# Pairwise outer products with batch norm: long rows as tiles of one sample, tiles in order of store

## The chip, the core and the metric

The kernel runs on one core of a Trainium2 chip. TensorE multiplies matrices, VectorE (DVE), ScalarE (ACT) and GpSimd (POOL) work element by element, SyncE (SP) issues the transfers, and 16 DMA engines carry them out. The metric is the time of one execution on the device, in microseconds (us); lower is better.

## The reference, cut to what matters

```python
B, F = 1024, 39            # r_xi, r_xj: (1024, 39, 16) float32
rows, cols = np.tril_indices(39, k=-1)      # 741 pairs (row > col)
cross = xj[:, rows, :, None] * xi[:, cols, None, :]        # (1024, 741, 16, 16)
mean = jnp.mean(cross, axis=(0, 2, 3), keepdims=True)
var = jnp.mean(jnp.square(cross - mean), axis=(0, 2, 3), keepdims=True)
normed = (cross - mean) * rsqrt(var + 1e-5)
normed = normed * gamma[None, :, None, None] + beta[None, :, None, None]
out = normed[:, :, None, :, :] * W[None, None, :, :, :]
```

For each sample and each pair of fields (row r, column c < r) the kernel forms the 16x16 outer product of two vectors, normalizes it with that pair's statistics over all samples, applies gamma and beta, and multiplies it by W. Row r has r pairs. The output has 1024 x 741 x 256 floats, 777 MB; the inputs have 5.1 MB.

## The kernel before

The 128 partitions hold eight samples each (`NT` = 8). A short first part loads the inputs, computes the statistics of all pairs from sums and small matrix products, and leaves for each pair a scale s and a shift t in `st_sb`. Each output pair is then (s xi) outer xj + t, times W.

**Tiles and slots.** The results pass through one buffer, `y_sb`, with 152 slots for a pair (one KB per partition each). The list `tiles` has one entry for each piece of work: its rows, its first sample `t0`, its first slot, and a mark. Each tile holds T = 2 samples. A row r and the rows that fill up its lap, 38 - r and its neighbour, share the 152 slots; I call one filling of the buffer a lap. The order of the list is: row 19 (four tiles), rows 20 and 18 in turn, row 38, then for r = 37, 35, ... 23 and each two samples row r, row r - 1 and the group of the two short rows (38 - r, 39 - r), and last rows 21 and 17. The row r - 1 (and every other tile of rows 20 and 38) lies at the end of the buffer with its two samples in reversed order (the mark `slot`, read by `at_of`), although it is stored second.

**Work on a tile.** The main loop at the end of the kernel takes tile after tile. `scale_xi(n + 2)` makes s xi on GpSimd (L191) into one of two buffers of the pool `scaled`. `finish(n)` adds t and multiplies by W. `products(n + 1)` makes the outer products of the next tile. A product is one instruction for one sample and one of the 16 values of xj, over all pairs of the row (L168 on ScalarE, L170 on GpSimd): ScalarE makes the first `split`, GpSimd the others. GpSimd makes 4 of 16, 5 in rows over 33 (`LONG`), and 3 in rows 31 to 33 (`POOL_I_BESIDE`), whose laps hold rows 5 to 7, which GpSimd makes in one instruction a sample (L226, `OUTER` = 7). Rows 1 to 4 are made by VectorE (L207, L217).

In `finish`, VectorE adds and multiplies pair by pair in one instruction over the tile's samples (`stt`, L334). It leaves a few pairs to GpSimd: in rows over 33 eight pairs (`POOL_PAIRS_LONG`), whose t ScalarE adds (L318) and which GpSimd then multiplies by W in two instructions (L323); in shorter tiles 13% of the pairs, with both steps on GpSimd (L320, L323).

**Stores.** All stores go out on SP's queue, in the order of the program; `bounds` says after which pairs of a tile `finish` calls `store`. A store waits for the engines that wrote its pairs. A product of a later tile waits for the store that reads its slots. Nothing reorders instructions: each engine follows the program, and waits come from overlaps of what is read and written.

The first eight tiles have piece sizes of their own (`FIRST_PIECES`). Row groups' statistics are spread ahead of need (`due`, in tiles).

Of the kernel before, what the change touches and what calls it, by code (L numbers as in the profile page):

```python
# [7 lines left out]
F32 = mybir.dt.float32  # L8
# [6 lines left out]
T = 2  # L15
# [3 lines left out]
ONE, LONG, WHOLE = 30, 33, 36  # L19
FIRST_PIECES = (  # L20
    (0, 1, 3, 6, 10, 14, 19), (0, 4, 9, 14, 19), (0, 4, 11, 19), (0, 9, 19), (0, 10, 20), (0, 9, 18), (0, 10, 20), (0, 9, 18)
)


POOL_I, POOL_I_LONG, POOL_I_FIRST = 4, 5, (6, 6, 5)
POOL_SHARE, POOL_PAIRS_LONG, POOL_PAIRS_FIRST = 0.13, 8, 3

SHORT, OWN = 4, 1


OUTER, POOL_I_BESIDE = 7, 3


ROW_GROUPS = (
# [7 lines left out]
def tile_pair_outer_batchnorm(  # L42
# [16 lines left out]
    P = nc.NUM_PARTITIONS  # L59
    NB, F, E = xi.shape  # L60
    NT = NB // P
    EE = E * E
# [4 lines left out]

    half = T * (F - 1)
    mid = (F - 1) // 2
    tiles = [((mid,), t0, t0 // T * half // 2, 0) for t0 in range(0, NT, T)]  # L70
    slot = 0
    for r in (mid + 1, F - 1):
        for t0 in range(0, NT, T):
            tiles.append(((r,), t0, slot * (2 * half - T * r), slot))
            if r < F - 1:
                tiles.append(((F - 1 - r,), t0, half if slot else T * r, 0))
            slot ^= 1
# [5 lines left out]
    r = mid + 2  # L83
    for t0 in range(0, NT, 2 * T):
        tiles.append(((r,), t0, 0, 0))
        tiles.append(((r,), t0 + T, 2 * half - T * r, 1))
        tiles.append(((F - 1 - r,), t0, T * r, 0))
        tiles.append(((F - 1 - r,), t0 + T, T * (F - 1), 0))

    RAW = 1  # L90

# [55 lines left out]
    stt = nc.vector.scalar_tensor_tensor  # L147

    def view(n):
        rows, _, u, _ = tiles[n]  # L150
        return y_sb[:, u : u + T * sum(rows), :].rearrange("p (t n) e -> p t n e", t=T)

    def parts(n):
        at = 0
# [1 line left out]
            yield r, at, at + r  # L156
            at += r

    def at_of(n, t):
        return T - 1 - t if tiles[n][3] else t  # L160

    def product(n, r, at, engine, t, i, src):

        t0 = tiles[n][1]
        y = view(n)[:, at_of(n, t), at : at + r].rearrange("p n (i j) -> p n i j", j=E)[:, :, i, :]
        scale = xj_sb[:, t0 + t, r, i : i + 1]
        if engine is nc.scalar:
            nc.scalar.activation(y, src, AF.Copy, scale=scale)  # L168
        else:
            engine.tensor_scalar(y, src, scale, 1.0, ALU.mult, ALU.mult)  # L170
# [11 lines left out]
    xs_of = {}  # L182

    def scale_xi(n):
        rows, t0 = tiles[n][:2]
        if rows[-1] <= SHORT:
            return
        xs = scaled.tile([P, T, sum(rows), E], F32, tag="xs", name=f"xs_{rows[0]}_{t0}")
        for r, c0, c1 in parts(n):
            n0 = first[r]  # L190
            nc.gpsimd.tensor_tensor(  # L191
                xs[:, :, c0:c1, :],
                xi_sb[:, t0 : t0 + T, 0:r, :],
                s_sb[:, :, n0 : n0 + r, :].to_broadcast([P, T, r, E]),
                ALU.mult,
            )
        xs_of[n] = xs

    def products(n):

        t0 = tiles[n][1]
        xs = xs_of.pop(n, None)
        for r, c0, c1 in parts(n):
            outer = view(n)[:, :, c0:c1].rearrange("p t n (i j) -> p t n i j", j=E)
            if r <= SHORT:
                xs_r = scaled_short.tile([P, T, r, E], F32, tag="xs_short", name=f"xs_{r}_{t0}")
                nc.vector.tensor_tensor(  # L207
                    xs_r,
                    xi_sb[:, t0 : t0 + T, 0:r, :],
                    s_short[:, first[r] : first[r] + r]  # L210
                    .unsqueeze(1)
                    .unsqueeze(3)
                    .to_broadcast([P, T, r, E]),
                    ALU.mult,
                )
                for t in range(T):
                    nc.vector.tensor_tensor(  # L217
                        outer[:, t],
                        xs_r[:, t].unsqueeze(2).to_broadcast([P, r, E, E]),
                        xj_short[:, t0 + t, r - 1 : r, :].unsqueeze(3).to_broadcast([P, r, E, E]),  # L220
                        ALU.mult,
                    )
                continue
            if r <= OUTER:
                for t in range(T):
                    nc.gpsimd.tensor_tensor(  # L226
                        outer[:, t],
                        xs[:, t, c0:c1].unsqueeze(2).to_broadcast([P, r, E, E]),
                        xj_sb[:, t0 + t, r : r + 1, :].unsqueeze(3).to_broadcast([P, r, E, E]),
                        ALU.mult,  # L230
                    )
# [12 lines left out]
    def store(n, c0, c1, t_from=0, t_to=T):  # L244
        rows, t0 = tiles[n][:2]
        n0, r = first[rows[0]], sum(rows)

        whole = n >= len(FIRST_PIECES) and r <= WHOLE
        flipped = tiles[n][3]
        step = 1 if flipped or r > mid and (whole or c1 == r) else t_to - t_from  # L250
        for t in range(t_from, t_to, step):
            if whole and step == 1 and t == t_to - 1:
                if c1 < r:
                    continue
                c0 = 0
            nc.sync.dma_start(
                out_v[:, t0 + t : t0 + t + step, (n0 + c0) * EE : (n0 + c1) * EE],
                view(n)[:, at_of(n, t) : at_of(n, t) + step, c0:c1, :].rearrange("p t n e -> p t (n e)"),
            )

    def affine(n, pairs, engines=(nc.scalar, nc.gpsimd)):
# [25 lines left out]
    def bounds(n):  # L287
        if n < len(FIRST_PIECES):
            return FIRST_PIECES[n]
        rows = tiles[n][0]  # L290
        r = sum(rows)
        if r <= ONE or len(rows) > 1:
            return 0, r

        return 0, r // 2 + max(0, (WHOLE + 1 - r) * 3 // 2), r

    def finish(n):


        rows = tiles[n][0]  # L300
# [12 lines left out]
        for c0 in range(p0, p1, step):  # L313
            c1 = min(c0 + step, p1)
            for c in range(c0, c1):
                t_c = t_sb[:, n0 + c : n0 + c + 1]
                if long:
                    nc.scalar.activation(y[:, :, c, :], y[:, :, c, :], AF.Identity, bias=t_c)  # L318
# [4 lines left out]
            nc.gpsimd.tensor_tensor(  # L323
                y[:, :, c0:c1, :],
                y[:, :, c0:c1, :],
                w_sb.unsqueeze(1).to_broadcast([P, T, c1 - c0, EE]),
                ALU.mult,
            )

        size = 1 if n == RAW else T  # L330
        for t in range(0, T, size):
            for c0, c1 in zip(bounds(n), bounds(n)[1:]):
                for c in [*range(c0, min(c1, p0)), *range(max(c0, p1), c1)]:
                    stt(  # L334
                        y[:, t : t + size, c, :],
                        y[:, t : t + size, c, :],
                        t_sb[:, n0 + c : n0 + c + 1],
                        w_dve.to_broadcast([P, size, EE]),
                        ALU.add,
                        ALU.mult,  # L340
                    )
                store(n, c0, c1, t, t + size)
# [247 lines left out]
```

## Time and profile before

| | us |
|---|---|
| median of 3 runs | 1865.06 (1864.89 to 1865.09) |
| the profiled execution, its own time | 1865.3 |
| its span | 1863.6 |
| VectorE busy | 1713.5 (92%) |
| ScalarE busy | 1574.4 (84%) |
| GpSimd busy | 1530.3 (82%) |
| TensorE busy | 33.1 (2%) |

Busy time is the time in which an engine executes an instruction. The rows of groups give for each source line and shape the count, the busy time, the mean length of one and the idle time ahead of it with what ended it. The table of stretches gives the same for chosen pieces of the span. In the timeline a row is a run of like instructions, with its start, its length, and in brackets the engine's idle time before it and what ended that.

The waits, summed up by who waited for whom, begin with these (total us, times, longest):

```profile
ACT y_sb L168 <- DMA out_dram<-y_sb: 210.2, 82, 8.9
POOL xs L191 <- ACT y_sb L168: 171.1, 42, 8.7
POOL y_sb L323 <- ACT y_sb L318: 78.5, 20, 7.7
```

### The profile page before, as it was taken

How to read it: one execution, taken by the hardware profiler on the slowest of the kernel's cores; microseconds unless marked ns; L12 is line 12 of the kernel's file. 1: busy time of each engine (PE TensorE's matmuls, PEld its weight loads, DVE VectorE, ACT ScalarE, POOL GpSimd, SP SyncE). 2: the span in 40 equal slices, each digit the busy share in tenths (PEclk: the TensorE clock that was granted, in tenths of full speed). 3: DMA queues.
4: the chain of work that ended last, by engine and by line, in shares of the span. 5: the costliest groups of instructions: out<-in, count | busy, mean ns of one | idle time of the engine just before them, and what ended most of it. 6: DMA issues, size and time to landing. Idle time of an engine off the chain costs nothing. (4 is left out here: it accounts for less than half of the span.)

```text
span 1863.6 us, 9245 instructions
## 1 busy us (share of the span) xinstructions
PE 33.1 (2%) x212; PEld 32.3 (2%) x212; DVE 1713.5 (92%) x2642; ACT 1574.4 (84%) x3130; POOL 1530.3 (82%) x1627
## 2 busy tenths in 40 slices
PE   7000000000000000000000000000000000000000
PEld 6000000000000000000000000000000000000000
DVE  8999889898999999999999999989998999999994
ACT  8999889888888777777877989899988998999981
POOL 9999778777877688889888888879878888888882
PEclk7555555555555555555555555555555555555555
DMA  7999999999999999999999999999999999999999
GB/s 294 395 422 423 428 426 412 427 428 436 427 427 427 414 416 428 427 425 423 429 428 433 409 428 418 433 427 428 428 431 428 428 435 426 420 419 426 426 427 386
DMA packets 46822, 783.60 MB, mean 420 GB/s; under 512 B 4512, under 2 KB 5152, under 8 KB 12704
## 3 DMA queue, kind: packets, MB, share of 16 engines
q1 hardware_dynamic: 46464, 782.53, 98.7%
q10 hardware_dynamic: 288, 0.48, 0.1%
q14 instruction: 69, 0.57, 0.1%
q8 instruction: 1, 0.02, 0.0%
HBM read 6.00 MB, written 776.99 MB: 420 GB/s over the span
## 5 line engine op out<-in xcount | busy, mean ns | idle before, releaser
L334 DVE SCALAR_TENSOR_TENSOR y_sb<-y_sb,st_sb,w_dve 128x512 f32<-128x512 f32 (+1 forms) x2515 | 1652.3, 739 | 115.2 <-issue 61.1
L168 ACT ACTIVATE y_sb<-xs,xj_sb 128x576 f32<-128x576 f32 (+23 forms) x2930 | 1451.3, 587 | 241.6 <-DMA out_dram<-y_sb 210.2
L323 POOL TENSOR_TENSOR y_sb<-y_sb,w_sb 128x2048 f32<-128x2048 f32 (+2 forms) x131 | 508.5, 3888 | 86.1 <-ACT y_sb L318 78.5
L170 POOL TENSOR_SCALAR y_sb<-xs,xj_sb 128x320 f32<-128x320 f32 (+21 forms) x1006 | 556.9, 576 | 9.8 <-DMA out_dram<-y_sb 9.7
L191 POOL TENSOR_TENSOR xs<-xi_sb,st_sb 128x640 f32<-128x640 f32 (+33 forms) x135 | 182.9, 1362 | 194.0 <-ACT y_sb L168 171.1
L320 POOL TENSOR_SCALAR y_sb<-y_sb,st_sb 128x512 f32<-128x512 f32 x287 | 193.5, 691 | 6.9 <-ACT y_sb L168 6.9
L318 ACT ACTIVATE y_sb<-y_sb,st_sb 128x512 f32<-128x512 f32 x160 | 100.2, 708 | 3.8 <-POOL y_sb L170 2.1
L226 POOL TENSOR_TENSOR y_sb<-xs,xj_sb 128x1280 f32<-128x1280 f32 (+2 forms) x24 | 66.5, 2801 | 0.0
L217 DVE TENSOR_TENSOR y_sb<-xs,ps 128x256 f32<-128x256 f32 (+3 forms) x32 | 24.8, 818 | 0.6
L513 PE MATMUL ps<-y_sb 38*128 38x38 f32 (+37 forms) x76 | 15.3, 378 | 2.4 <-DVE y_sb L499 2.4
L513 PEld LDWEIGHTS ps<-y_sb 38*128 38x128 f32 x76 | 15.2, 309 | 2.5 <-POOL y_sb L170 2.5
L170 POOL TENSOR_SCALAR y_sb<-xi_sb,xj_sb 128x304 f32<-128x304 f32 x24 | 11.9, 513 | 0.0
L279 DVE TENSOR_TENSOR y_sb<-y_sb,w_dve 128x2048 f32<-128x2048 f32 (+4 forms) x6 | 10.8, 1840 | 0.5 <-POOL y_sb L272 0.5
L390 DVE TENSOR_REDUCE y_sb<-y_sb 128x38 f32<-128x608 f32 x14 | 10.4, 780 | 0.0
L272 POOL TENSOR_SCALAR y_sb<-y_sb,st_sb 128x512 f32<-128x512 f32 x9 | 7.0, 793 | 1.6 <-ACT y_sb L168 1.6
L387 ACT ACTIVATE y_sb<-xj_sb 128x608 f32<-128x608 f32 x8 | 5.7, 709 | 1.1 <-DMA xj_sb<-in_r_xj_dram 0.7
L387 ACT ACTIVATE y_sb<-xi_sb 128x608 f32<-128x608 f32 x8 | 5.7, 706 | 1.1 <-DMA xi_sb<-in_r_xi_dram 0.8
L270 ACT ACTIVATE y_sb<-y_sb,st_sb 128x512 f32<-128x512 f32 x9 | 6.5, 804 | 0.1
L405 PE MATMUL ps<-xi_sb,y_sb 128*128 128x152 f32 x40 | 5.8, 295 | 0.1
L405 PEld LDWEIGHTS ps<-xi_sb,y_sb 128*128 128x128 f32 x40 | 5.5, 193 | 0.3 <-issue 0.3
L427 PE MATMUL ps<-y_sb 128*128 128x128 f32 x24 | 5.5, 428 | 1.0 <-POOL y_sb L345 1.0
L390 DVE TENSOR_REDUCE y_sb<-xi_sb 128x38 f32<-128x608 f32 x2 | 1.6, 785 | 4.0 <-DMA xi_sb<-in_r_xi_dram 4.0
(43 smaller groups left out, 54.1 us busy)
## 6 DMA issues: line engine op xcount, KB each, us to landing
out_dram<-y_sb SPq DMA_DIRECT2D x20, 2944.0 KB, 15.4
out_dram<-y_sb SPq DMA_DIRECT2D x24, 2432.0 KB, 12.8
out_dram<-y_sb SPq DMA_DIRECT2D x16, 3456.0 KB, 17.2
out_dram<-y_sb SPq DMA_DIRECT2D x12, 3968.0 KB, 19.6
out_dram<-y_sb SPq DMA_DIRECT2D x10, 4608.0 KB, 15.5
out_dram<-y_sb SPq DMA_DIRECT2D x12, 3840.0 KB, 20.5
out_dram<-y_sb SPq DMA_DIRECT2D x16, 2816.0 KB, 16.8
out_dram<-y_sb SPq DMA_DIRECT2D x12, 3072.0 KB, 14.4
```

Source lines behind the costliest of these rows:

```text
L168: nc.scalar.activation(y, src, AF.Copy, scale=scale)
L170: engine.tensor_scalar(y, src, scale, 1.0, ALU.mult, ALU.mult)
L191: nc.gpsimd.tensor_tensor(xs[:, :, c0:c1, :], xi_sb[:, t0 : t0 + T, 0:r, :], s_sb[:, :, n0 : n0 + r, :].to_broadcast([P, T, r, E]), ALU.mult,)
L217: nc.vector.tensor_tensor(outer[:, t], xs_r[:, t].unsqueeze(2).to_broadcast([P, r, E, E]), xj_short[:, t0 + t, r - 1 : r, :].unsqueeze(3). ...
L226: nc.gpsimd.tensor_tensor(outer[:, t], xs[:, t, c0:c1].unsqueeze(2).to_broadcast([P, r, E, E]), xj_sb[:, t0 + t, r : r + 1, :].unsqueeze(3 ...
L318: nc.scalar.activation(y[:, :, c, :], y[:, :, c, :], AF.Identity, bias=t_c)
L320: nc.gpsimd.tensor_scalar(y[:, :, c, :], y[:, :, c, :], t_c, 1.0, ALU.add, ALU.mult)
L323: nc.gpsimd.tensor_tensor(y[:, :, c0:c1, :], y[:, :, c0:c1, :], w_sb.unsqueeze(1).to_broadcast([P, T, c1 - c0, EE]), ALU.mult,)
L334: stt(y[:, t : t + size, c, :], y[:, t : t + size, c, :], t_sb[:, n0 + c : n0 + c + 1], w_dve.to_broadcast([P, size, EE]), ALU.add, ALU.mult,)
L387: nc.scalar.activation(squares[x][:, t], sources[x][:, t], AF.Square, scale=scales[x])
L390: nc.vector.tensor_reduce(moment(x, k, t, t + 1), field(x, k)[:, t : t + 1], AX.X, ALU.add)
L513: nc.tensor.matmul(ps[:, :, first[r] - n0 : first[r] - n0 + r], pick[:, r - 1, :], stq[:, :, 0:r], start=True, stop=True,)
```

## The change

- The mark and the reversal are gone. `lap` lays the tiles of a lap one behind the other in the order in which they are stored.
- In rows 34 to 38 a tile holds one sample (`size` 1) and is stored whole. Of its pairs 10 go by ScalarE and GpSimd, in two parts of 5, where it was 8 for two samples.
- `OUTER` is 5: rows 6 and 7 are made by single products on ScalarE and GpSimd.
- GpSimd makes 5 of 16 products in tiles of two short rows (`POOL_I_GROUP`), and 4 in rows 31 to 33.
- `bounds` and `store` cut the other tiles in new places: two thirds, or half in the first tile of row 33; only a sample's own pieces are sent singly.

```diff
-POOL_I, POOL_I_LONG, POOL_I_FIRST = 4, 5, (6, 6, 5)
-POOL_SHARE, POOL_PAIRS_LONG, POOL_PAIRS_FIRST = 0.13, 8, 3
+POOL_I, POOL_I_LONG, POOL_I_GROUP, POOL_I_FIRST = 4, 5, 5, (6, 6, 5)
+POOL_SHARE, POOL_PAIRS_LONG, POOL_PAIRS_FIRST = 0.13, 10, 3
-OUTER, POOL_I_BESIDE = 7, 3
+OUTER = 5
...
+    def lap(*members):
+        u = 0
+        for rows, t0, size in members:
+            for t in range(t0, t0 + T, size):
+                tiles.append((rows, t, size, u))
+                u += size * sum(rows)
+        assert u <= 2 * half
...
     for r in range(F - 2, mid + 2, -2):
         for t0 in range(0, NT, T):
-            tiles.append(((r,), t0, 0, 0))
-            tiles.append(((r - 1,), t0, 2 * half - T * (r - 1), 1))
-            tiles.append(((F - 1 - r, F - r), t0, T * r, 0))
+            lap(
+                ((r,), t0, 1 if r > LONG else T),
+                ((r - 1,), t0, 1 if r - 1 > LONG else T),
+                ((F - 1 - r, F - r), t0, T),
+            )
...
             elif r > LONG:
                 split = E - POOL_I_LONG
+            elif len(tiles[n][0]) > 1:
+                split = E - POOL_I_GROUP
             else:
-                split = E - (POOL_I_BESIDE if SHORT < F - 1 - r <= OUTER else POOL_I)
-            for t in range(T):
+                split = E - POOL_I
+            for t in range(size):
...
+        parted = n >= len(FIRST_PIECES) and c1 - c0 < sum(rows)
+        step = 1 if n >= len(FIRST_PIECES) else t_to - t_from
+        if parted and c0 == 0:
+            t_to = t_from + 1
         for t in range(t_from, t_to, step):
-            if whole and step == 1 and t == t_to - 1:
-                if c1 < r:
-                    continue
+            if parted and t:
                 c0 = 0
...
-        if r <= ONE or len(rows) > 1:
+        if size == 1 or len(rows) > 1 or r <= ONE and (r < ONE or t0):
             return 0, r
-        return 0, r // 2 + max(0, (WHOLE + 1 - r) * 3 // 2), r
+        if r == LONG and t0 == 0:
+            return 0, r // 2, r
+        return 0, 2 * r // 3, r
```

More of the change, by code (lines that the diff above doesn't have):

```diff
@@ L69, in tile_pair_outer_batchnorm @@
     mid = (F - 1) // 2
[L70 to L77, printed above, removed]
+    tiles = [((mid,), t0, T, t0 // T * half // 2) for t0 in range(0, NT, T)]
+    def lap(*members):
[5 more added lines that the diff above has]
+        assert u <= 2 * half
+    for t0 in range(0, NT, 2 * T):
+        lap(*(((x,), t, T) for t in (t0, t0 + T) for x in (mid + 1, mid - 1)))
+    for t0 in range(0, NT, 2 * T):
+        lap(((F - 1,), t0, 1), ((F - 1,), t0 + T, 1))
     for r in range(F - 2, mid + 2, -2):
         for t0 in range(0, NT, T):
-            tiles.append(((r,), t0, 0, 0))
-            tiles.append(((r - 1,), t0, 2 * half - T * (r - 1), 1))
-            tiles.append(((F - 1 - r, F - r), t0, T * r, 0))
-    r = mid + 2
+            lap(
[3 more added lines that the diff above has]
+            )
     for t0 in range(0, NT, 2 * T):
[L85 to L88, printed above, removed]
+        lap(*(((x,), t, T) for t in (t0, t0 + T) for x in (mid + 2, mid - 2)))
     RAW = 1
@@ L149, in view @@
     def view(n):
-        rows, _, u, _ = tiles[n]
-        return y_sb[:, u : u + T * sum(rows), :].rearrange("p (t n) e -> p t n e", t=T)
+        rows, _, size, u = tiles[n]
+        return y_sb[:, u : u + size * sum(rows), :].rearrange("p (t n) e -> p t n e", t=size)
     def parts(n):
@@ L157, in parts @@
             at += r
[L159 to L160 removed]
     def product(n, r, at, engine, t, i, src):
         t0 = tiles[n][1]
[L165 removed]
+        y = view(n)[:, t, at : at + r].rearrange("p n (i j) -> p n i j", j=E)[:, :, i, :]
         scale = xj_sb[:, t0 + t, r, i : i + 1]
@@ L184, in scale_xi @@
     def scale_xi(n):
-        rows, t0 = tiles[n][:2]
+        rows, t0, size = tiles[n][:3]
         if rows[-1] <= SHORT:
             return
-        xs = scaled.tile([P, T, sum(rows), E], F32, tag="xs", name=f"xs_{rows[0]}_{t0}")
+        xs = scaled.tile([P, size, sum(rows), E], F32, tag="xs", name=f"xs_{rows[0]}_{t0}")
         for r, c0, c1 in parts(n):
@@ L192, in scale_xi @@
                 xs[:, :, c0:c1, :],
-                xi_sb[:, t0 : t0 + T, 0:r, :],
-                s_sb[:, :, n0 : n0 + r, :].to_broadcast([P, T, r, E]),
+                xi_sb[:, t0 : t0 + size, 0:r, :],
+                s_sb[:, :, n0 : n0 + r, :].to_broadcast([P, size, r, E]),
                 ALU.mult,
@@ L199, in products @@
     def products(n):
-        t0 = tiles[n][1]
+        t0, size = tiles[n][1:3]
         xs = xs_of.pop(n, None)
@@ L242, in products, with store @@
                     product(n, r, c0, engine, t, i, xs[:, t, c0:c1])
[L244 to L250, printed above, removed]
+    def store(n, c0, c1, t_from=0, t_to=None):
+        rows, t0, size = tiles[n][:3]
+        n0 = first[rows[0]]
+        t_to = t_to or size
+        parted = n >= len(FIRST_PIECES) and c1 - c0 < sum(rows)
+        step = 1 if n >= len(FIRST_PIECES) else t_to - t_from
+        if parted and c0 == 0:
+            t_to = t_from + 1
         for t in range(t_from, t_to, step):
-            if whole and step == 1 and t == t_to - 1:
-                if c1 < r:
-                    continue
+            if parted and t:
                 c0 = 0
@@ L257, in store @@
                 out_v[:, t0 + t : t0 + t + step, (n0 + c0) * EE : (n0 + c1) * EE],
-                view(n)[:, at_of(n, t) : at_of(n, t) + step, c0:c1, :].rearrange("p t n e -> p t (n e)"),
+                view(n)[:, t : t + step, c0:c1, :].rearrange("p t n e -> p t (n e)"),
             )
@@ L289, in bounds @@
             return FIRST_PIECES[n]
-        rows = tiles[n][0]
+        rows, t0, size, _ = tiles[n]
         r = sum(rows)
-        if r <= ONE or len(rows) > 1:
+        if size == 1 or len(rows) > 1 or r <= ONE and (r < ONE or t0):
             return 0, r
-        return 0, r // 2 + max(0, (WHOLE + 1 - r) * 3 // 2), r
+        if r == LONG and t0 == 0:
+            return 0, r // 2, r
+        return 0, 2 * r // 3, r
     def finish(n):
-        rows = tiles[n][0]
+        rows, _, each = tiles[n][:3]
         n0, r = first[rows[0]], sum(rows)
@@ L325, in finish @@
                 y[:, :, c0:c1, :],
-                w_sb.unsqueeze(1).to_broadcast([P, T, c1 - c0, EE]),
+                w_sb.unsqueeze(1).to_broadcast([P, each, c1 - c0, EE]),
                 ALU.mult,
             )
-        size = 1 if n == RAW else T
-        for t in range(0, T, size):
+        size = 1 if n == RAW else each
+        for t in range(0, each, size):
             for c0, c1 in zip(bounds(n), bounds(n)[1:]):
```

## The prediction

> **What bounds the kernel now.** I read the page first: the slices, then the queues.
>
> ```profile
> DMA  7999999999999999999999999999999999999999
> GB/s 294 395 422 423 428 426 412 427 428 436 427 427 427 414 416 428 427 425 423 429 428 433 409 428 418 433 427 428 428 431 428 428 435 426 420 419 426 426 427 386
> q1 hardware_dynamic: 46464, 782.53, 98.7%
> HBM read 6.00 MB, written 776.99 MB: 420 GB/s over the span
> ```
>
> The output alone is 776.99 MB, and from the third slice on the DMA engines are full. No engine sets the end: the chain of waits ends in a 23 us transfer. So an edit counts only by (a) what a byte costs on the DMA engines and (b) the moments in which they have nothing queued. For (b) I cut the run into stretches of equal work, one per two rows (busy us and count of PE, PEld, DVE, ACT, POOL; clock; DMA share; GB/s). The six are rows 37/36, 35/34, then 29/28, 27/26, 25/24 and 23/22.
>
> ```profile
> 270.00:457.00 187.00, 0.00 (x0) 0.00 (x0) 168.16 (x266) 160.72 (x245) 146.99 (x106) 0.50 1.00 424
> 457.00:641.00 184.00, 0.00 (x0) 0.00 (x0) 176.34 (x268) 152.96 (x239) 140.24 (x105) 0.50 1.00 428
> 1016.00:1203.00 187.00, 0.00 (x0) 0.00 (x0) 173.10 (x263) 168.15 (x385) 155.60 (x197) 0.50 0.99 423
> 1203.00:1390.00 187.00, 0.00 (x0) 0.00 (x0) 177.85 (x275) 171.56 (x394) 155.64 (x200) 0.50 1.00 429
> 1390.00:1577.00 187.00, 0.00 (x0) 0.00 (x0) 171.74 (x261) 168.59 (x386) 154.14 (x197) 0.50 1.00 429
> 1577.00:1763.00 186.00, 0.00 (x0) 0.00 (x0) 172.24 (x262) 168.16 (x385) 152.67 (x195) 0.50 0.99 424
> ```
>
> 429 GB/s is what this kernel reaches when nothing is missing. A lap, one filling of y_sb's 152 pair slots (19.92 MB), takes 46.5 us at that rate. Against 429, rows 29/28 lose (429-423)/429 x 187 = 2.6 us and rows 23/22 lose (429-424)/429 x 186 = 2.2 us. The same table gave 423 GB/s for rows 33/32 (641 to 829 us): 2.6 us lost there. Short windows on the holes show them empty:
>
> ```profile
> 219.50:220.50 1.00, 0.00 (x0) 0.00 (x0) 1.00 (x3) 1.00 (x3) 1.00 (x3) 0.50 0.46 195
> 296.00:297.00 1.00, 0.00 (x0) 0.00 (x0) 0.96 (x4) 1.00 (x3) 1.00 (x2) 0.50 0.26 105
> 1652.00:1654.00 2.00, 0.00 (x0) 0.00 (x0) 0.65 (x1) 2.00 (x6) 2.00 (x5) 0.50 0.66 276
> ```
>
> The timeline around the last one shows why:
>
> ```profile
> 1639.77 20.45 ACT L168 ACTIVATE y_sb<-xs,xj_sb 128x256 f32<-128x256 f32 x43
> 1642.80 1.39 POOL L191 TENSOR_TENSOR xs<-xi_sb,st_sb 128x704 f32<-128x704 f32 x1 [7.64 <-ACT y_sb L168]
> 1651.46 4.40 POOL L170 TENSOR_SCALAR y_sb<-xs,xj_sb 128x368 f32<-128x368 f32 x8
> 1655.89 4.70 DVE L334 SCALAR_TENSOR_TENSOR y_sb<-y_sb,st_sb,w_dve 128x512 f32<-128x512 f32 x7 [3.23 <-POOL y_sb L170]
> ```
>
> GpSimd waits 7.64 us for ScalarE to finish the short-row group, because scaled xi has two buffers; then it needs 13 us until its products for row 23 are done, and VectorE stands idle 3.23 us. The lap is 46.8 us where the DMA needs 46.5.
>
> The groups by shape give prices. Their means include an overlap with the next instruction; busy divided by count, or start to start in the records, is what a row of them costs.
>
> ```profile
> L334 DVE SCALAR_TENSOR_TENSOR y_sb<-y_sb,st_sb,w_dve 128x512 f32<-128x512 f32 x2481 | 1639.0, 742 | 115.2 <-issue 61.1 <-POOL y_sb L170 46.9 <-POOL xs L191 7.0
> L318 ACT ACTIVATE y_sb<-y_sb,st_sb 128x512 f32<-128x512 f32 x160 | 100.2, 708 | 3.8 <-POOL y_sb L170 2.1
> L334 DVE SCALAR_TENSOR_TENSOR y_sb<-y_sb,st_sb,w_dve 128x256 f32<-128x256 f32 x34 | 13.4, 476 | 0.0
> ```
>
> VectorE: 658 ns start to start for two samples of a pair, 392 ns for one (13.4/34 agrees). One sample each costs 784 for the same work.
>
> **What the Trainium skill says.** "VectorE: DVE Perf Modes", section on the TRN2 errata: the latency is paid per instruction, "a single large tile pays it once; many small tiles pay it per-tile". The trace agrees: 2 x 392 - 658 = 126 ns. "DMA: Bandwidth & Descriptors", Why small descriptors are slow: every packet carries a fixed overhead. The packet records agree: 3,072 bytes took 125 ns and 36,864 bytes 1,372 ns, so 11.6 ns a packet and 27.1 bytes/ns beyond. "Perfetto Trace Analysis", Optimization Strategy: consistent bubbles can mean that no buffer is free for the next tile; the hole at 1652 us, repeated 46.8 us apart, fits that.
>
> **The change, part by part.**
>
> *Stores.* Counting store rows in the two programs, 39,680 packets become 36,224 (a sample of rows 34 to 38 goes out whole). 3,456 x 11.6 ns / 16 engines = -2.5 us. Nothing hides it where the DMA is full. SP issues 264 stores for 262: nothing.
>
> *Rows 38 to 36.* A tile is one sample. For row 38 the DMA needs 11.58 us (8 packets an engine, 38,912 bytes). VectorE: 28 x 0.392 = 11.0. ScalarE: 10 instructions at L318 of 256 elements, whose price is the nearest L168 row (128x256: 0.399 start to start) 4.0, plus 11 products x 0.693 = 7.6, plus hand-offs of 0.2: 11.8. GpSimd: wait for five L318 and the hand-off 2.2, two multiplications of 1,280 elements (between 2.33 at 1,024 and 3.42 at 1,536: 2.88 each) 5.75, five products 3.73: 11.7. Scaled xi (1.2) lies in the wait. So this ring of ScalarE and GpSimd is 0.2 us a tile too slow, 1.7 over eight tiles. A lap of rows 37/36: ring 46.3, VectorE 2 x (27 + 26) x 0.392 = 41.6 plus 4.4 for rows 1 and 2: 46.0; DMA 46.5. From the records of issues and packets, some 4 us are queued when row 38 begins, so no hole is due here. The holes that before has from 172 to 300 us (missing shares 0.26, 0.54, 0.17, 0.74 in four 1 us windows) come from half-lap tiles waiting for each other's slots; quarter laps have more air: -1.7 us.
>
> *Rows 35/34.* VectorE per lap: 2 x (25 + 24) x 0.392 = 38.4, plus 7 x 0.658 = 4.6 and 4.7 for the products of rows 3 and 4: 47.7, where before it has 53 x 0.658 + 9.3 = 44.2. The DMA needs 46.6, so VectorE becomes the bound, 1.1 us a lap, 4.4 in four laps; about 3 us of queued transfer absorb part: +1.4 us. ScalarE (45) and GpSimd (46) don't bind.
>
> *The step to row 33* (two samples a tile again, first store 16 pairs of one sample). VectorE reaches that store after 16 x 0.658 = 10.6 us with 8.7 us queued: 1.9 missing; it adds 4.9, the rest comes 8.6 later: 3.7 missing. With 0.5 later on, 6.1 for this stretch, against 2.6 before: +3.5 us.
>
> *Short-row groups, rows 9 to 16.* ScalarE makes 11 of 16 products, not 12: 4 x 0.39 = 1.6 us less per lap for rows 15/16, 1.25 for 9/10; GpSimd's four more (1.8) lie in its 7.64 us wait. The wait at L191 ends 1.2 us sooner and with it VectorE's: the lap needs 45.6, less than the DMA. Both holes go: -2.6 - 2.2 = -4.8 us. What is late next is the transfer itself.
>
> *At nothing:* GpSimd's fourth product in rows 31 to 33 and rows 6 and 7 as single products (ScalarE has 131 of 188 us busy there, GpSimd loses two L226 of 2.8 or 3.2 us a lap for ten small products); slot order and the lost reversal (each tile still follows the tile that held its slots a lap earlier). If that cover failed, it is a ring wait as above, at most 1 us a lap. The first 75 us and the last transfer don't change: the first eight tiles keep their pieces, and VectorE ends 23 us before the last byte.
>
> *Sum:* -2.5 - 1.7 + 1.4 + 3.5 - 4.8 = -4.1 us. The profiled execution, 1865.3 us (span 1863.6), becomes 1861.2; the median of the runs, 0.2 lower, 1861.0.
>
> **Rivals.** *The ring of the one-sample tiles is slower than worked out.* Three hand-offs a tile, taken at 0.04 to 0.09 us as in the trace; if each costs 0.1 more, 24 tiles of rows 38 to 36 lose 7.2 us. With the 1.7 above, less 0.8 spare in rows 37/36 and 2.1 queued, 6.0 us are missing, and rows 35/34 begin without their 3 us: +9.0, so 1870. For it: the ring is within 0.2 us of the DMA time. Against: none of the present hand-offs is that long. It decides from about 0.3 us a tile; below 0.25 it is not slower by 0.2%. *Nothing starves in rows 35 to 33:* if a deeper queue is built up by then, the 4.9 us don't come and before's 2.6 there goes as well: about -12, 1853. For it: free slots allow some 14 us of queue beyond the current store. Against: nothing fills it while the engines need as long as the DMA. *The groups' relief doesn't reach the DMA:* the next wait takes its place at once; then -4.1 + 4.8 = +0.7: 1866.
>
> **How the numbers follow.** Forecast 0.45 (its own range 1857 to 1865), slower ring 0.17, nothing starves 0.20, no relief 0.18. A measurement tells 0.2%, 3.7 us, from no change: bounds 1861.3 and 1868.8. Faster: a bit over half of the forecast (0.26), the third case and a little of the last: 0.48. Slower: most of the ring case and a remnant: 0.18. The rest, 0.34, lies between. The range 1852 to 1870 takes in packets alone with all holes gone below, and the slow ring above.
>
> **What would show it.** GB/s of rows 29/28 and 23/22 at 428 or more, and no hole repeating there (step right); VectorE over 98% busy in rows 35/34 with a hole where row 33 begins; no wait of ScalarE for stores over 3 us in rows 38 to 34; 11.7 to 11.9 us between stores of row 38. It is wrong if row 38's stores stand over 12.1 us apart, or if rows 35/34 run at 428 GB/s without VectorE being full.

## The result and the profile after

The changed kernel takes 1874.92 us (median of 4 runs, 1874.61 to 1875.1) against 1865.05 us before on the same chip: ratio 1.0053, 95% interval 1.0035 to 1.007. It is 9.9 us slower, where 4.1 us less was forecast. The profiled span is 1873.4 us, against 1863.6.

In the source after, the lines have moved: products are L169 (ScalarE) and L171 (GpSimd), scaled xi is L192, ScalarE's "add t" for the GpSimd pairs is L322, GpSimd's multiplication by W is L327, VectorE's pair-by-pair work is L338.

From the page of the changed kernel, the slices of transfer rate, the store queue and the sum:

```profile
GB/s 293 396 422 432 433 433 427 427 415 430 377 426 414 385 407 429 427 428 428 430 429 423 433 427 431 425 434 426 434 428 412 426 426 428 418 418 426 428 426 377
q1 hardware_dynamic: 43040, 782.53, 98.0%
HBM read 6.00 MB, written 776.99 MB: 418 GB/s over the span
```

The same 776.99 MB go out in fewer packets (43,040, where it was 46,464), but the queue is busy for 98.0% of the span, not 98.7%. A slice is 47 us long; the low ones, 415, 377, 414, 385 and 407, are the ninth to the fifteenth, 375 to 703 us.

The table of stretches, in the columns used in the prediction. The rows are row 38, rows 37/36, 35/34, 33/32, 29/28 and 23/22:

```profile
170.00:270.00 100.00, 0.00 (x0) 0.00 (x0) 96.06 (x248) 99.27 (x179) 91.25 (x67) 0.50 1.01 434
270.00:457.00 187.00, 0.00 (x0) 0.00 (x0) 179.44 (x449) 179.74 (x332) 164.76 (x127) 0.50 0.99 424
457.00:641.00 184.00, 0.00 (x0) 0.00 (x0) 180.16 (x419) 176.31 (x326) 160.40 (x129) 0.50 0.97 414
641.00:829.00 188.00, 0.00 (x0) 0.00 (x0) 180.88 (x275) 142.28 (x280) 160.29 (x177) 0.50 0.97 411
1016.00:1203.00 187.00, 0.00 (x0) 0.00 (x0) 175.85 (x267) 165.58 (x371) 161.76 (x213) 0.50 1.00 429
1577.00:1763.00 186.00, 0.00 (x0) 0.00 (x0) 172.66 (x263) 161.63 (x370) 159.90 (x212) 0.50 0.99 423
```

Row 38 runs at 434 GB/s. The loss lies in two stretches, rows 35/34 (428 before, 414 now) and 33/32 (423 and 411). Rows 29/28 went from 423 to 429 as forecast (what did it is told below), rows 23/22 did not (424 and 423).

Short windows tell two kinds of holes apart. Three in the lossy stretches and one in the late rows, in the same columns:

```profile
500.50:504.50 4.00, 0.00 (x0) 0.00 (x0) 4.00 (x12) 4.00 (x10) 3.07 (x2) 0.50 0.00 0
647.00:649.50 2.50, 0.00 (x0) 0.00 (x0) 2.50 (x5) 2.50 (x5) 2.31 (x4) 0.50 0.00 0
655.50:658.00 2.50, 0.00 (x0) 0.00 (x0) 2.50 (x5) 1.34 (x6) 2.42 (x2) 0.50 0.00 0
1613.00:1615.00 2.00, 0.00 (x0) 0.00 (x0) 0.55 (x1) 2.00 (x5) 2.00 (x5) 0.50 0.64 272
```

In the first three the DMA share is 0.00: all 16 engines have nothing to do for 2.5 to 4 us. In the last it is 0.64: some are idle, others still work. I call the first kind all idle and summed it from the packet records: the time from 75 us up to the last store in which no packet of 512 bytes or more is under way. It is 1.5 us before and 10.6 us after. This difference, 9.1 us, is nearly the whole change of the span (9.8). In the changed kernel the all-idle moments are at 500.5 us (4.0 us), 551.8 (0.5), 599.5 (0.5), 647.3 (2.6) and 655.3 (3.0).

**Why the queue was empty at 500 us.** ScalarE and GpSimd form a ring: each waits once a tile for the other. The prediction let scaled xi (1.2 us of GpSimd) lie in GpSimd's wait for ScalarE. The timeline of GpSimd in the changed kernel, beside the group of rows 3 and 4:

```profile
474.97 1.15 POOL L192 TENSOR_TENSOR xs<-xi_sb,st_sb 128x560 f32<-128x560 f32 x1
477.30 5.77 POOL L327 TENSOR_TENSOR y_sb<-y_sb,w_sb 128x1280 f32<-128x1280 f32 x2 [1.17 <-ACT y_sb L322]
483.01 1.16 POOL L192 TENSOR_TENSOR xs<-xi_sb,st_sb 128x560 f32<-128x560 f32 x1
484.13 3.58 POOL L171 TENSOR_SCALAR y_sb<-xs,xj_sb 128x560 f32<-128x560 f32 x5
```

The first L192 does lie ahead of a wait (1.17 us remain of it). The second doesn't: a group of VectorE rows is a step of the loop in which GpSimd only scales, so its L192 comes straight behind the multiplications and ahead of the products for which ScalarE waits. ScalarE's timeline at that moment:

```profile
479.06 7.28 ACT L169 ACTIVATE y_sb<-xs,xj_sb 128x560 f32<-128x560 f32 x11
487.74 4.10 ACT L322 ACTIVATE y_sb<-y_sb,st_sb 128x256 f32<-128x256 f32 x10 [1.40 <-POOL y_sb L171]
```

Once a lap ScalarE waits 1.4 us here. Beside the group of rows 1 and 2 the order is the same (L192 between L327 and L171 from 292.61 us on) and the wait 1.28 us. With it the ring needs about 46.3 + 1.4 = 47.7 us for a lap of rows 37/36, and the DMA 46.5; VectorE comes to these groups every 47.75 us (294.84, 342.59, 390.34). The queue shrinks accordingly. Each store leaves 16 landing marks, one from each DMA engine. When row 37's first store of a lap is issued, the first and the last mark of the store before it are still 5.0 and 7.4 us away in the first lap, 1.8 and 4.1 in the second, 0.4 and 3.0 in the third; in the fourth the first mark is already there and the last 1.9 us away. Rows 35/34, in which VectorE is slower than the DMA, then begin with 0.5 to 1.6 us.

### The profile page after: what moved, and what is told of

Same layout as the page of the kernel before. It is cut to its first block, busy times and chain, and to the rows that moved or that the text cites. A ratio compares the mean times of both kernels' runs of the same rounds, so it can differ in the third digit from the quotient of the medians.

```text
span 1873.4 us, 10367 instructions
## 1 busy us (share of the span) xinstructions
PE 33.1 (2%) x212; PEld 32.3 (2%) x212; DVE 1753.1 (94%) x3122; ACT 1644.5 (88%) x3450; POOL 1607.7 (86%) x1847
## 3 DMA queue, kind: packets, MB, share of 16 engines
q1 hardware_dynamic: 43040, 782.53, 98.0%
HBM read 6.00 MB, written 776.99 MB: 418 GB/s over the span
## 5 line engine op out<-in xcount | busy, mean ns | idle before, releaser
L338 DVE SCALAR_TENSOR_TENSOR y_sb<-y_sb,st_sb,w_dve 128x512 f32<-128x512 f32 (+1 forms) x2995 | 1691.7, 646 | 85.5 <-POOL y_sb L171 50.1
L169 ACT ACTIVATE y_sb<-xs,xj_sb 128x288 f32<-128x288 f32 (+23 forms) x3010 | 1460.8, 576 | 162.0 <-DMA out_dram<-y_sb 142.6
L171 POOL TENSOR_SCALAR y_sb<-xs,xj_sb 128x576 f32<-128x576 f32 (+24 forms) x1182 | 628.7, 556 | 5.1 <-DMA out_dram<-y_sb 5.0
L327 POOL TENSOR_TENSOR y_sb<-y_sb,w_sb 128x1280 f32<-128x1280 f32 (+4 forms) x171 | 558.6, 3277 | 57.7 <-ACT y_sb L322 50.1
L192 POOL TENSOR_TENSOR xs<-xi_sb,st_sb 128x608 f32<-128x608 f32 (+30 forms) x155 | 186.6, 1211 | 161.1 <-ACT y_sb L169 147.6
L322 ACT ACTIVATE y_sb<-y_sb,st_sb 128x256 f32<-128x256 f32 x400 | 164.0, 494 | 19.6 <-POOL y_sb L171 18.3
L227 POOL TENSOR_TENSOR y_sb<-xs,xj_sb 128x1280 f32<-128x1280 f32 x8 | 18.7, 2358 | 0.0
L171 POOL TENSOR_SCALAR y_sb<-xi_sb,xj_sb 128x304 f32<-128x304 f32 x24 | 11.9, 518 | 0.0
L272 ACT ACTIVATE y_sb<-y_sb,st_sb 128x512 f32<-128x512 f32 x9 | 6.5, 800 | 0.1
L431 PEld LDWEIGHTS ps<-y_sb 128*128 128x128 f32 x24 | 5.2, 331 | 1.0 <-POOL y_sb L349 1.0
```

Of the source, the lines that this page charges most:

```text
L192: nc.gpsimd.tensor_tensor(xs[:, :, c0:c1, :], xi_sb[:, t0 : t0 + size, 0:r, :], s_sb[:, :, n0 : n0 + r, :].to_broadcast([P, size, r, E]), ...
L227: nc.gpsimd.tensor_tensor(outer[:, t], xs[:, t, c0:c1].unsqueeze(2).to_broadcast([P, r, E, E]), xj_sb[:, t0 + t, r : r + 1, :].unsqueeze(3 ...
L327: nc.gpsimd.tensor_tensor(y[:, :, c0:c1, :], y[:, :, c0:c1, :], w_sb.unsqueeze(1).to_broadcast([P, each, c1 - c0, EE]), ALU.mult,)
L338: stt(y[:, t : t + size, c, :], y[:, t : t + size, c, :], t_sb[:, n0 + c : n0 + c + 1], w_dve.to_broadcast([P, size, EE]), ALU.add, ALU.mult,)
```

## The experiments

Each kernel is compared with the kernel before on its own chip (1865.05 to 1865.75 us); the interval is that of the ratio. "All idle" is the sum defined above.

| kernel | us | ratio, 95% interval | all idle, us |
|---|---|---|---|
| before | 1865.05 | | 1.5 |
| after | 1874.92 | 1.0053, 1.0035 to 1.007 | 10.6 |
| e1_late_xs | 1870.39 | 1.0028, 1.0017 to 1.0039 | 6.7 |
| e2_two_samples | 1861.67 | 0.9981, 0.9974 to 0.9989 | 0.4 |
| e3_two_samples_35_34 | 1867.83 | 1.0014, 1.0007 to 1.0021 | 5.5 |
| e4_group_4 | 1874.83 | 1.0052, 1.0036 to 1.0069 | 10.7 |
| e5_late_xs_two_samples_35_34 | 1864.62 | 0.9996, 0.9987 to 1.0004 | 2.0 |
| e6_late_xs_less_vector | 1864.54 | 0.9996, 0.9987 to 1.0004 | 2.1 |
| e7_before_new_shares | 1863.47 | 0.999, 0.9981 to 0.9999 | 0.8 |
| e8_two_samples_old_cuts | 1864.67 | 0.9996, 0.9988 to 1.0005 | 2.4 |
| e9_two_samples_more_packets | 1874.29 | 1.0047, 1.0032 to 1.0062 | 0.0 |
| e10_two_samples_old_shares | 1863.09 | 0.9987, 0.9981 to 0.9994 | 1.0 |
| e11_eight_pairs | 1890.3 | 1.0133, 1.0116 to 1.015 | 23.5 |
| e12_two_samples_short_groups | 1860.9 | 0.9974, 0.9964 to 0.9984 | 0.5 |

The time less the last column lies between 1861 and 1865 us in all rows but e9, e11 and e12. Apart from e9 the order of the kernels is nearly that of the last column. That holds for large differences. Those below some 3 us it does not explain: e2 is 3.6 us faster than before with only 1.1 us less all idle.

### Is it the second L192? (e1_late_xs)

```diff
-            if n + 2 < len(tiles):
+            late = tiles[n][0][-1] <= SHORT
+            if n + 2 < len(tiles) and not late:
                 scale_xi(n + 2)
...
                 products(n + 1)
+            if n + 2 < len(tiles) and late:
+                scale_xi(n + 2)
```

> Theory A (GpSimd's place in the ring): in a lap of rows 37/36 the second scaled xi (1.2 us) stands between the multiplication and the products, because the group of rows 1 and 2 gives GpSimd no work; so the ring needs 47.7 us a lap, not 46.3, and empties the queue before rows 35/34 come. Moved behind the products of the next tile, it lies in a wait again: no hole over 0.4 us from 300 to 460 us, the 4.3 us hole at 500 us down to about 1, in all some 5 to 8 us less than the changed kernel, 1867 to 1870. Rival B (VectorE alone): rows 35/34 keep 47.7 us a lap and the holes there and at row 33 stay; within 2 us of the changed kernel, 1873 to 1875.

1870.39, 4.5 us less than after and 0.4 above the range of theory A. The edit moves the second L192 in rows 37/36 and in rows 35/34. The table of stretches of this kernel, rows 37/36 and 35/34:

```profile
270.00:457.00 187.00, 0.00 (x0) 0.00 (x0) 182.47 (x458) 184.10 (x339) 169.06 (x130) 0.50 1.00 429
457.00:641.00 184.00, 0.00 (x0) 0.00 (x0) 181.22 (x416) 175.83 (x325) 163.57 (x133) 0.50 0.97 417
```

Rows 37/36 now run at 429 GB/s (424 in after), without a hole from 150 to 457 us. VectorE comes to the groups of rows 1 and 2 every 46.64 us (294.88, 341.52, 388.16), 1.1 us sooner than in after, and rows 35/34 begin with 1.7 to 4.8 us queued. So the misplaced L192 is shown, and its worth is 4.5 us. Rows 35/34 remain slow at 417: there another engine binds.

### Two samples a tile throughout, or only in rows 35/34 (e2_two_samples, e3_two_samples_35_34)

In e2 the order, the rule for the cuts and the shares of the products stay as after; row 38 has two samples too, and a long tile gives away 8 pairs, not 10. In e3 rows 38 to 36 stay at one sample and 10 pairs, rows 35/34 have two and 8.

```diff
-POOL_SHARE, POOL_PAIRS_LONG, POOL_PAIRS_FIRST = 0.13, 10, 3
+POOL_SHARE, POOL_PAIRS_LONG, POOL_PAIRS_FIRST = 0.13, 8, 3
...
-                ((r,), t0, 1 if r > LONG else T),
-                ((r - 1,), t0, 1 if r - 1 > LONG else T),
+                ((r,), t0, T),
+                ((r - 1,), t0, T),
```

> All long rows back to tiles of two samples and 8 pairs, the order of slots, the groups' shares and the cuts of the stores as in the changed kernel. If the one-sample tiles are the whole loss (A and B alike): holes from 150 to 690 us as in the kernel before (about 4 us), packets nearly as before, so 1861 to 1865. If the order of slots costs something by itself: over 1867.

1861.67 us: faster than before by 3.6 and than after by 13.3. All of the loss comes with the one-sample tiles, and this version beats both kernels. Rows 35/34 in its table of stretches:

```profile
457.00:641.00 184.00, 0.00 (x0) 0.00 (x0) 176.38 (x268) 151.17 (x236) 140.42 (x106) 0.50 1.00 428
```

VectorE is busy 176.4 us here and in before, 180.2 in after, and the transfer is full again.

```diff
-                ((r,), t0, 1 if r > LONG else T),
-                ((r - 1,), t0, 1 if r - 1 > LONG else T),
+                ((r,), t0, 1 if r > LONG + 2 else T),
+                ((r - 1,), t0, 1 if r - 1 > LONG + 2 else T),
```

> Rows 35 and 34 alone back to two samples and 8 pairs; rows 38 to 36 stay as changed. Rival B (VectorE's 47.7 us a lap there is the loss): the holes at 500, 551, 599 and 646 to 658 us go down to 1 or 2 us in all, 1862 to 1865, and e1 does little. Theory A alone (the ring of rows 37/36 is the loss): those rows' three holes (2.3 us) stay and the first lap of rows 35/34 still starves, 1867 to 1870.

1867.83, 7.1 us less than after, but 6.2 more than e2. The time lies in the range of theory A alone, but not for its reason: the three holes of rows 35/34 are gone, and a hole of 5.5 us has come. A window on the place where row 35 begins:

```profile
454.20:458.20 4.00, 0.00 (x0) 0.00 (x0) 4.00 (x7) 4.00 (x7) 4.00 (x2) 0.50 0.00 0
```

The step from one-sample to two-sample tiles has moved from row 33 to row 35, and its hole with it: VectorE and ScalarE are at work and the transfer has nothing, because the first store of two-sample tiles comes late, at 458.80 us. The two steps are not quite alike. In after VectorE works through the step to row 33 without a pause. Here it stands idle ahead of the first tile of two samples, until ScalarE has made the 22 products of both (432.50 to 446.95 us):

```profile
447.03 17.86 DVE L338 SCALAR_TENSOR_TENSOR y_sb<-y_sb,st_sb,w_dve 128x512 f32<-128x512 f32 x27 [3.84 <-issue]
```

After the step rows 35/34 run at 428 GB/s.

### Does a filled queue carry the step? (e5_late_xs_two_samples_35_34)

These are e1's and e3's edits together; a part of each is shown.

```diff
+                ((r,), t0, 1 if r > LONG + 2 else T),
+                ((r - 1,), t0, 1 if r - 1 > LONG + 2 else T),
...
+            if n + 2 < len(tiles) and late:
+                scale_xi(n + 2)
```

> e1 and e3 together: the late scaled xi and two samples a tile in rows 35 and 34. If the idle moment at the step from one-sample to two-sample tiles (5.5 us with all DMA engines idle in e3, where next to nothing is queued at the step) depends on what is queued then: e1 had no hole up to 457 us, so some 4 to 5 us are queued, the idle moment shrinks to 1 or 2 us, and the time is 1862 to 1864. If the step costs 5 us whatever is queued: 1866 to 1868.

1864.62, 3.2 less than e3 and 0.6 above the range. There is no hole until 451 us, and the idle time of all engines at the step falls from 5.5 to 2.0 us. The queue carries part of the step, not all of it. VectorE's wait of 3.84 us ahead of the first two-sample tile is there as in e3.

### Is it VectorE in rows 35/34? (e6_late_xs_less_vector)

```diff
-                for c in [*range(c0, min(c1, p0)), *range(max(c0, p1), c1)]:
+                for c in [*range(c0, min(c1, p0)), *range(max(c0, p1), c1 - 4 * (LONG < r < LONG + 3))]:
```

On top of e1's edit.

> e1, with the last four pairs of each tile of rows 35 and 34 left as they are before t and W (VectorE leaves out four of 25 or 24 instructions a tile, so those pairs of the output are not the reference's). Theory: VectorE's 47.7 us a lap is what starves the transfers in rows 35/34; at 41.4 us a lap the holes at 497, 547, 594 us go, the queue fills, and the idle moments at row 33 (5.6 us) shrink below 2: 1864 to 1866. Rival (a sample stored whole is too coarse, whatever VectorE needs): the holes stay, 1869 to 1871.

1864.54, 5.9 us less than e1. The table of stretches over rows 35/34 and the first window at the step:

```profile
457.00:641.00 184.00, 0.00 (x0) 0.00 (x0) 163.53 (x364) 178.19 (x330) 163.63 (x133) 0.50 0.99 422
636.00:640.00 4.00, 0.00 (x0) 0.00 (x0) 4.00 (x7) 2.98 (x5) 4.00 (x7) 0.50 0.25 102
```

VectorE's busy time in the stretch falls from 181 to 164 us, and e1's holes at 496.9, 546.6 and 594.3 us are gone. What is left is the step to row 33 (share 0.25 at 636 us), which lies within the stretch and holds its mean at 422. So VectorE's 47.7 us lap did starve the transfer in rows 35/34.

### Eight pairs on GpSimd instead of ten (e11_eight_pairs)

```diff
-POOL_SHARE, POOL_PAIRS_LONG, POOL_PAIRS_FIRST = 0.13, 10, 3
+POOL_SHARE, POOL_PAIRS_LONG, POOL_PAIRS_FIRST = 0.13, 8, 3
```

> The changed kernel with 8 pairs of a long tile on ScalarE and GpSimd, not 10. By sums of instructions VectorE needs 11.8 us a tile in row 38, 49.1 us a lap in rows 37/36 and 50.8 in rows 35/34, where the transfers need 46.7: 2.4 and 4.1 us lost in each of four laps, 26 us, with the step to row 33 as it is (6 us): about 1895. If the ring of ScalarE and GpSimd is what counts in rows 37/36 and VectorE only later: 1880 to 1886.

1890.3, between the two expectations. VectorE's timeline in rows 37/36, where a row holds the pairs of a lap:

```profile
300.16 46.71 DVE L338 SCALAR_TENSOR_TENSOR y_sb<-y_sb,st_sb,w_dve 128x512 f32<-128x512 f32 x117
349.24 46.71 DVE L338 SCALAR_TENSOR_TENSOR y_sb<-y_sb,st_sb,w_dve 128x512 f32<-128x512 f32 x117
```

From start to start 49.08 us, without an idle stretch; summed from the prices it is 2 x (29 + 28) x 0.392 + 4.4 = 49.1. The prices of the prediction hold: two pairs more a tile on VectorE cost 3.1 us a lap, and the ten pairs are needed with one-sample tiles.

### The shares of the short rows (e4_group_4, e7_before_new_shares, e10_two_samples_old_shares)

```diff
-POOL_I, POOL_I_LONG, POOL_I_GROUP, POOL_I_FIRST = 4, 5, 5, (6, 6, 5)
+POOL_I, POOL_I_LONG, POOL_I_GROUP, POOL_I_FIRST = 4, 5, 4, (6, 6, 5)
```

> GpSimd makes 4 of 16 products in the groups of short rows again, all else as changed. The prediction's step (holes of rows 29/28 and 23/22 closed by the fifth product, 4.8 us): 1879 to 1880, with holes back in rows 29/28. If the lap there is set by the transfers anyway: within 1.5 us of the changed kernel.

1874.83, as after (0.1 less). The fifth product, for which the prediction took 4.8 us off, is worth nothing here. Nor do holes come back in rows 29/28: they run at 428 GB/s with the old share.

```diff
-OUTER, POOL_I_BESIDE = 7, 3
+OUTER, POOL_I_GROUP = 5, 5
...
-                split = E - (POOL_I_BESIDE if SHORT < F - 1 - r <= OUTER else POOL_I)
+                split = E - (POOL_I_GROUP if len(tiles[n][0]) > 1 else POOL_I)
```

> The kernel before, with the new shares of the products alone (rows 6 and 7 as single products, 5 of 16 on GpSimd in groups of two rows, 4 in rows 31 to 33). The prediction's step: the late holes close and 4.8 us are gained, 1860 to 1861. What e4 suggests: the holes fall on DMA engines that are ahead of the slowest, and nothing is gained, 1864 to 1866; e2's 3.6 us then come from the order of slots or the cuts of the stores.

These shares alone, in the kernel before: 1863.47, 1.8 us less. It lies between the two expectations and decides only that the gain is well below 4.8. All idle goes from 1.5 to 0.8 us, mostly at 663, 1064 and 1158 us.

For e10 the edit is e2's with the old shares:

```diff
-OUTER = 5
+OUTER, POOL_I_BESIDE = 7, 3
...
-                split = E - POOL_I
+                split = E - (POOL_I_BESIDE if SHORT < F - 1 - r <= OUTER else POOL_I)
```

`POOL_I_GROUP` is 4 there as well.

> e2 with the shares of the kernel before (rows 6 and 7 in one instruction a sample, 4 of 16 on GpSimd in the groups, 3 in rows 31 to 33): order of slots and cuts alone. If shares and order add up (e7 gained 1.8 us): 1863.5. If the order and the cuts already give all: 1861 to 1862.

1863.09, 1.4 more than e2. The stretch of rows 29/28 with all the old shares:

```profile
1016.00:1203.00 187.00, 0.00 (x0) 0.00 (x0) 175.63 (x267) 171.04 (x393) 157.25 (x200) 0.50 1.01 430
```

So the holes of rows 29/28 close without the fifth product. In the order of before all the new shares reach only 426 GB/s there (e7), and in the new order with the old cuts it is 430 again (e8 below), which points to the order of the slots. All the shares together are worth 1.4 to 1.8 us (e10, e7), the fifth product alone 0.1 (e4). What e10 loses lies in rows 33/32 (421 GB/s, where e2 has 425, and 0.5 us all idle at 688 us). That points to the other two shares, single products for rows 6 and 7 and 4 of 16 in rows 31 to 33; no run changed them alone.

### Why the late holes cost so little (e12_two_samples_short_groups)

```diff
                 for i in range(E):
+                    if len(tiles[n][0]) > 1 and r > 8 and 6 <= i < split:
+                        continue
```

On top of e2.

> The kernel of e2_two_samples, in which ScalarE leaves out 5 of its 11 products a row and sample in the groups of rows 9 to 16 (those pairs keep old values in 5 of 16 columns): 20 instructions a lap fewer, some 8 us, so that neither GpSimd at L192 nor VectorE behind it can be late there. In e2_two_samples VectorE waits 3.2 to 4.1 us a lap for GpSimd in rows 23/22, and the holes from 980 to 1750 us sum up to 5.8 us of missing engine time / 16. Theory A (the late holes lie on DMA engines that are ahead of the slowest one and cost nothing): VectorE's waits for GpSimd go and so do these holes, but the time stays within 1 us of 1861.7, and the first and last landing of a store drift further apart. Theory B (the late holes cost what they miss, as the prediction summed): 1856 to 1858. If VectorE's waits stay as they are, the run decides nothing.

1860.9, 0.8 less than e2. In e2 VectorE waited 4.07, 3.26 and 3.24 us for GpSimd's products in rows 23/22, and so it does in after:

```profile
1617.61 43.54 DVE L338 SCALAR_TENSOR_TENSOR y_sb<-y_sb,st_sb,w_dve 128x512 f32<-128x512 f32 x66 [4.06 <-POOL y_sb L171]
1664.39 43.54 DVE L338 SCALAR_TENSOR_TENSOR y_sb<-y_sb,st_sb,w_dve 128x512 f32<-128x512 f32 x66 [3.24 <-POOL y_sb L171]
```

VectorE's timeline of e12, where ScalarE has some 7 us less to do in such a lap (136.0 us busy in rows 23/22, in e2 162.9):

```profile
1626.81 43.79 DVE L340 SCALAR_TENSOR_TENSOR y_sb<-y_sb,st_sb,w_dve 128x512 f32<-128x512 f32 x66 [2.97 <-ACT y_sb L169]
1673.54 17.86 DVE L340 SCALAR_TENSOR_TENSOR y_sb<-y_sb,st_sb,w_dve 128x512 f32<-128x512 f32 x27 [2.94 <-ACT y_sb L169]
```

VectorE still idles 3 us a lap and the lap is as long (46.73 us here, 46.78 in after). Only what it waits for has changed: now for ScalarE, and ScalarE for a store, as its timeline shows.

```profile
1671.03 7.21 ACT L169 ACTIVATE y_sb<-xs,xj_sb 128x240 f32<-128x240 f32 x18 [7.03 <-DMA out_dram<-y_sb]
```

So ScalarE's work was not the bound. The landing marks of the stores name what is: in e12 the last of a store's 16 marks comes 6 to 8 us after the first in these rows (1655.47 and 1661.47 us for one store of the group), in e2 3.2 to 5.7. The ends of the last packets in e12:

```
... 1851.74 1851.76 1851.79 1851.96 1852.08 1852.27 1852.34
1852.72 1853.37 1854.02 1854.66 1855.31 1855.95 1856.60 1857.24 1857.89
```

From 1852.72 on they come 0.65 us apart, which is the time of one packet of that store: a single DMA engine works off its rest when the others are done. A store frees its slots when that one is done too: the store for which ScalarE waits until 1671.03 us has its first mark at 1664.90 and its last at 1670.95. In after ScalarE goes on at 1638.03 and 1684.82, and the last marks are at 1637.94 and 1684.74. Against e2 the first landing of the last store is 3.2 us earlier (1851.96 and 1855.16) and the last only 1.1 (1858.34 and 1859.48). The holes from 1040 to 1850 us, missing engine time / 16, shrink from 5.8 to 3.1 us, and most of that is gained by engines that then wait for the slowest. The run speaks for theory A: 2.7 us of holes went, and the time fell by 0.8 us (1.3, if each kernel is compared with before on its own chip). It doesn't settle it, since VectorE's waits stayed as long and about half of the holes stayed. e4 points the same way: its holes after 829 us are 1.2 us larger than those of after, and its time is 0.1 us less.

### The cuts and the packets (e8_two_samples_old_cuts, e9_two_samples_more_packets)

```diff
-        if size == 1 or len(rows) > 1 or r <= ONE and (r < ONE or t0):
+        if r <= ONE or len(rows) > 1:
             return 0, r
-        if r == LONG and t0 == 0:
-            return 0, r // 2, r
-        return 0, 2 * r // 3, r
+        return 0, r // 2 + max(0, (WHOLE + 1 - r) * 3 // 2), r
```

On top of e2.

> e2 with the cuts of the tiles where the kernel before has them (half and a bit, none at row 30). If the new cuts give e2 its gain: back to 1864 to 1865. If the order of slots does: within 1 us of e2, 1861 to 1862.5.

1864.67, 3.0 more than e2, with a new hole at 179.6 to 182 us, where row 38 begins (2.2 us all idle). The two-thirds cuts are part of e2's gain; e10, with the old shares and the new cuts, is still some 2 us faster than before. e8 itself, with the new order and shares, gains only 0.6 us over before, less than the shares alone (e7, 1.8). How the rest splits between order and cuts was not separated.

```diff
+            cuts = (c0, (c0 + c1) // 2, c1) if step == 1 and c1 - c0 > 12 else (c0, c1)
+            for a0, a1 in zip(cuts, cuts[1:]):
```

Each part is then one transfer; on top of e2, 65,536 store packets where e2 has 38,784.

> e2 with every single-sample store over 12 pairs sent as two transfers: 65,536 packets for 38,784, the same bytes. At the prediction's price (11.6 ns a packet on one of 16 engines): 26,752 x 11.6 / 16 = 19.4 us more than e2, 1881. If that price is hidden (packets overlap, or the time isn't set by it): under 6 us more.

1874.29, 12.6 more than e2, between the two theories. The packets' own time, summed and divided by 16, rose by 24.3 us (1841.5 to 1865.9), and the holes of e2 were filled: at no moment were all engines idle. The last store lands on its first engine at 1863.55 us and on its last at 1871.84. "DMA: Bandwidth & Descriptors" in the Trainium skill (Why small descriptors are slow) has a fixed overhead for each packet; these runs agree, with 24.3 x 16 / 26,752 = 14.5 ns a packet, but a gain or loss in the sum of packet times is not one in time of the same size.

## Why the prediction was wrong, step by step

*Packets, -2.5 us.* The packets' time / 16 fell by 3.0 us (1842.86 to 1839.88), so the count was right and the price a little low. That it shows in full in the kernel's time was wrong. Up to the last landing, with at most 16 packets counted at a moment, the engines' busy time fell by 2.0 us, and their idle time rose by 11.7: 9.1 all idle, and 2.7 in partial holes and at the end, where the slowest DMA engine lags more (first to last landing 3.0 us before, 4.3 after). These 2.7 took up the gain.

*Row 38.* Right. ScalarE's steps start 11.81 us apart (179.06, 190.88, 202.69), as worked out; the holes of before from 150 to 275 us are gone (missing 1.08, then 0.03).

*Rows 37/36, "Scaled xi (1.2) lies in the wait".* This step failed first. It holds for every tile but the one beside a VectorE group, where two L192 follow each other and one stands ahead of GpSimd's products. A lap took 47.75 us, not 46.3. e1 takes this one wait away: its laps take 46.64 us, and the kernel gains 4.5 us.

*Rows 35/34, +1.4 us.* The lap of 47.7 us on VectorE was right to the digit (the holes begin 47.7 us apart: 550.9, 598.6, 646.4), and e6 shows that it binds. What failed is "about 3 us of queued transfer absorb part": the step above had used them up. The loss was 5.0 us all idle, not 1.4. e1 still loses 2.75 us of engine time at the start of these rows, so the queue assumed was too large even without the misplaced L192.

*The step to row 33, +3.5 us.* Nearly right: 6.1 us were summed, 6.8 were missing, of which 5.5 with all engines idle. e3 moves the step and its hole goes with it; e5 and e6 leave 2 us of it all idle with a fuller queue. Why a fuller queue doesn't carry all of it stayed open. VectorE's wait ahead of the first two-sample tile (3.84 us in e3 and e5, 1.51 in e6, none in after) may be part of it.

*Short-row groups, -4.8 us.* Failed on both counts. In rows 23/22 VectorE's wait for GpSimd is as long as it was (3.23 before, 3.24 after), although GpSimd took over products: what starts that round is the landing of a store on the slowest DMA engine. The 429 GB/s of rows 29/28 came true by luck: e4 (428) and e10 (430) have them without the fifth product, and the runs point to the order of the slots. And the holes counted were mostly holes on the engines ahead: the all-idle time of before after 829 us is only 0.6 us, so by that measure there was little to win. e4 measured 0.1 us for the fifth product.

*At nothing.* Rows 6 and 7 as single products and the fourth product in rows 31 to 33 were put at nothing; the place of e10's holes points to a gain of some 1.4 us from them.

*The sum.* In all-idle time the stretches add up: 0.8 us less ahead of rows 35/34, 5.0 more in them, 5.4 more at the step, 0.6 less in the late rows, 9.0 in all. Where -1.7, +1.4, +3.5 and -4.8 were forecast, both losses were too small and both gains too large.

*The signs.* Row 38's stores stood 11.8 us apart, ScalarE did not wait for a store in rows 38 to 34, and VectorE was busy 97.9% in rows 35/34 with a hole where row 33 begins, all about as named. Neither sign of being wrong came, for none of them looked at the laps of rows 37/36. Two readings of the profile before were off, without weight: VectorE's work ends 26 us ahead of the last landing (1836.3 and 1862.5), not 23, and the 23 us transfer in the chain is followed by 20 us of work on ScalarE and VectorE.

*The rivals.* The slower ring came nearest, in its mechanism (rows 35/34 begin without their queue) and its time (1870). Its price was sought in the hand-offs, which were as short as taken; the ring was longer by a whole instruction, at one place a lap. "The groups' relief doesn't reach the DMA" was true at the same time. The forecast took the rivals one at a time; in hindsight two together, 1870 + 4.8 = 1874.8, would have met the result.

## What to carry to other kernels

When the work of a loop is split over engines in a ring, write out the order of the instructions once for each kind of step, not only for the common one: a step that gives an engine little to do can put its preparatory work in front of what others wait for. A slack of some us that covers several slow stretches is spent once, so carry it along as a running balance from stretch to stretch. And before a partly idle resource is counted as lost time, ask whether all of its units were idle: here the large differences in time went with the holes of all 16 DMA engines, not with the partial ones.

## What the hardware showed that I had not expected

The 16 DMA engines that share one store don't keep step. In stretches without an all-idle moment the first and the last landing of a store drift apart: in after from 0.2 us at 664 us to 7.0 us at 1451 us, in e9, which has no all-idle moment, to 9.1 us near its end. They come together again where all engines ran empty (1.0 us before the hole at 655 us, 0.2 after it). Small holes that stop only the engines ahead cost little (e12: 2.7 us fewer of them, 0.8 us gained). What makes one engine slower than the others the runs don't tell.
